# Pairing the chunks of a two-part matrix product so that its fp16 halves lie in runs of sixteen

## The chip, the core and the metric

The kernel runs on one core of a Trainium2 chip. Its time is the device time of one execution in microseconds, the median of several runs. The engines are named as in the profile: PE multiplies matrices (PEld is its loading of weights), DVE, ACT and POOL work on vectors, SP issues nearly all DMAs. Each engine works through its own list of instructions in order, and semaphores tie the lists together.

## The reference

The input x is 4 batches of 1024 tokens of 512 channels. It is normalized, and the result goes into two branches whose outputs are added to x:

```
xn  = layernorm(x)
# time mix, 704 hidden channels
k   = (xn + (shift(xn) - xn) * mix_k) @ Wk.T ;  r likewise with mix_r and Wr
s_t = s_(t-1) * exp(-exp(decay)) + relu(k_t) ;  a = layernorm((s * r) @ Wv.T) * gamma + beta
# feed-forward, 2048 hidden channels
d   = fp16(gelu(fp16(xn) @ W0.T + bias0)) ;     e = fp16(d @ W1.T + bias1)
out = x + a + e
```

## The kernel before

The tokens are cut into eight blocks of 512 (i = 0 to 7; block 1 is the second one). The tile of 128 x 512 is the unit of nearly all work.

**Feed-forward.** The hidden 2048 channels are 16 chunks of 128 (n = 0 to 15). For a chunk, `up` (L843) makes the hidden product pd, 512 columns wide, from four groups of input channels. The weights are in two parts, a high one in fp32r (w0h, against the inputs xf) and a low one in fp16 (w0l, against the fp16 inputs x16), so pd takes four fp32r and four fp16 products, in this order. ACT turns pd into d16 (gelu, L866) and copies it to d in fp32r (L869). `down` (L875) adds the chunk's share to the four output sums pe (one for each 128 tokens): four fp16 products of d16 with the low part of W1, then four fp32r products of d with the high part. The weights come back from DRAM in each block: w1 by `load_w1`, w0l by `load_w0l`.

**The loop.** Iteration n of a block runs, in this order on PE: `up` for the chunk two further on (its high, then its low products), `down` for chunk n (low, then high), and then a piece of the time mix. A piece is a three-pass product of k or r (L693 and L444: sums pa and pb, 12 products), a half pass (ph, 8 products) or, at n = 12 to 15, an output product for 128 tokens (`out_three_pass`, L790 to L800: sums oa and ob, 17 products). All of these are fp32r. So one iteration has 8 fp16 products in a row and else fp32r.

What follows a piece on DVE and ACT is emitted in the next iteration (`followers`): a<-pa on ACT (L705), y<-pb,a on DVE (L706), then the scan (L585) for k, or the gating g (L602) and the split of g into three parts hg, lg and mg (L278, L336, L338, L340) for r. An output piece is followed by oy (L805), its statistics, scaling and residual (L777, L782, L783). The gelu of the iteration is emitted between the first step of these works and the rest of them. Jobs of the next block are woven in between: its normalization and transposes, the mixing at n = 10, 12, 13 and 14 (L420, L424) and, behind each mixing, the split of the mixed inputs of one of the four channel groups into hk, lk and mk (`split_xk`). After iteration 15 DVE rounds the four sums pe to e (L833), which frees their banks of PSUM for the next block.

**Order and buffers.** Inside the loop the order of PE, DVE, ACT and SP is the order in which the code emits it. PSUM has four banks for pd, pa, pb, ph, oa and ob in turn, and four for pe. Nearly all tiles of SBUF come from one pool of equal buffers under the tag "q" (`part`, QS buffers): w0h, the parts h, l and m of the inputs, the states g and their parts, the parts of Wv. A new tile takes a buffer that an earlier one had, and its first writer waits for that tile's last reader. A few tags have their own buffers: kr (weights of the three-pass products, 6), w1 (2), w1l (2), w0l (2), d and d16 (3 each), xf (4), h16 (8).

**The tail.** The last block keeps the `down` of its last four chunks for the end: token groups 0 and 1 whole, 512 wide, groups 2 and 3 in two halves of 256 columns (`end_by_columns`, L886). There each fp16 product of a chunk is followed by its fp32r product.

Of the kernel before, what the change touches and what calls it, by code (L numbers as in the profile page):

```python
# [10 lines left out]
F16 = mybir.dt.float16  # L11
# [6 lines left out]
P = 128  # L18
# [4 lines left out]
def time_mix_and_gelu_ffn(  # L23
# [32 lines left out]
    nc = tc.nc  # L56
    B, T, C = x.shape
# [3 lines left out]
    NS = TB // P  # L61
    NC = C // P
    NN = N // P
    Q = 32
    QS = 62
    RAW_OUT = 1
    WV_FIRST = {0: 12, 1: 13, 2: 15, 3: 15, 5: 15}
    S = 4096.0
# [1 line left out]
    MASK = -4096  # L70
    OWN = dict(tag="q", bufs=QS)

# [5 lines left out]
    LAST = len(blocks) - 1  # L78
# [9 lines left out]

    def part(name, dtype=F32R, tag="q", bufs=QS):
        return wide.tile([P, TB], dtype, tag=tag, name=name, bufs=bufs)  # L90
# [112 lines left out]
    w0h, w0l, w0ls, w0l_pairs = {}, {}, {}, {}  # L203
# [18 lines left out]

    def load_w0l(i, n):
        if i > 1 or i == 1 and n >= G:
            w0ls[i, n] = part(f"w0l_{i}_{n}", F16, tag="w0l", bufs=2)
            g, k = divmod(n, G)
            src = w0l_dram[g][:, k].rearrange("p c k -> p (c k)")
            nc.sync.dma_start(w0ls[i, n], src)
# [19 lines left out]
    def load_w1(i, n):  # L248
        name = f"w1_{i}_{n}"
        if i == LAST and n >= NN - 2:  # L250
            w1 = [part(f"{name}_0"), pair(f"{name}_1")[0]]
        else:
            w1 = [
                part(f"{name}_0", tag="w1", bufs=2),
                part(f"{name}_1", F16, tag="w1l", bufs=2),
            ]
        if i == 0:
            split(*w1, w1_raw.pop(n))
        for p in range(2):
            sbuf, kept = as_stored(w1[p], p), as_stored(w1_dram[n][p], p)  # L260
            if i == 0:
                stores.append((kept, sbuf))
            else:
                nc.sync.dma_start(sbuf, kept)
        return w1
# [574 lines left out]
        queue.dma_start(out[b, rows, cols], z[:, cols])  # L840


    def up(i, n):  # L843
        pd = bank(f"pd_{i}_{n}")
        g, k = divmod(n, G)
        cols = slice(k * P, (k + 1) * P)
        low = w0ls.pop((i, n), None)
        for p in range(2):
            for c in range(NC):
                if p == 0:  # L850
                    w = w0h[c, g][:, cols]
                elif low is not None:
                    w = low[:, c * P : (c + 1) * P]
                else:
                    w = w0l[c, g][:, cols]
                nc.tensor.matmul(  # L856
                    pd, w, xf[c][p], start=(c == p == 0), stop=(c == NC - 1 and p == 1)
                )

        def after():  # L860
            if i == LAST and n >= NN - 2:
                d, d16 = part(f"d_{i}_{n}"), pair(f"d16_{i}_{n}")[0]
            else:
                d = part(f"d_{i}_{n}", tag="d", bufs=3)
                d16 = part(f"d16_{i}_{n}", F16, tag="d16", bufs=3)
            nc.scalar.activation(  # L866
                d16, pd, AF.Gelu, bias=b0_sb[:, n : n + 1], scale=1.0 / WS
            )
            nc.scalar.copy(d, d16)  # L869
            return d, d16  # L870

        return after


    def down(n, tiles, d, w1, first=0, end=lambda s: NN, sums=None, cols=slice(0, C)):  # L875
        for p in (1, 0):
            for s in tiles:
                nc.tensor.matmul(  # L878
                    (sums or pe)[s],
                    d[p][:, s * P : (s + 1) * P],  # L880
                    w1[p][:, cols],
                    start=(n == first and p == 1),
                    stop=(n == end(s) - 1 and p == 0),
                )

    def end_by_columns(s, chunks, base):  # L886
        first = NN - len(chunks)
        for half in range(2):
            cols = slice(half * C // 2, (half + 1) * C // 2)
            sum_ = bank(f"end_{s}_{half}")[:, : C // 2]  # L890
            for n, operands in chunks:
                down(n, [s], *operands, first=first, sums={s: sum_}, cols=cols)
            finish(LAST, s, rounded(LAST, s, sum_, cols, base), cols)

    AHEAD = 2
# [21 lines left out]
    def several(fn, *calls):  # L917
        for args in calls:
            fn(*args)

    engines = {e.engine for e in (nc.tensor, nc.vector, nc.scalar, nc.sync)}
    with tc.manual_schedule(engines=engines):
        for kind in range(2):
            begun[kind, 0] = begin_kr(kind, 0, lambda name: part(name, F32))
        first_x16(0)
        for h in range(FIRST):
            finished(raw_k(0, h, pks[h])())
        for c in range(1, NC):
            first_x16(c)
        xf = ffn_input(0)  # L930
        finished(raw_r(0, 0)())
        several(split_w0, (0, 0), (0, 1))
        finished(raw_r(0, 1)())
        several(split_w0, (0, 2), (0, 3))
        w1s = [load_w1(0, n) for n in range(AHEAD)]
        gated_last = raw_r(0, 2)
        several(split_w0, (1, 0), (1, 1))
        several(split_kr, (1, 0, 0), (1, 1, 0))
        finished(gated_last())
        waiting = []  # L940
        for n in range(AHEAD):
            waiting.append((up(0, n)(), w1s[n]))
            split_w0(1, 2 + n)
        store_weights()
    behind.close()

    followers = []
    e16s = []
    with tc.manual_schedule(engines=engines):
        for i in range(len(blocks)):  # L950
            j = i + 1
            tail = 4 if i == LAST else 0
# [106 lines left out]
            for n in range(NN):  # L1059
                ahead = n + AHEAD  # L1060
                if ahead == NN and j <= LAST:
                    xf = next_xf
                nxt = (i, ahead) if ahead < NN else (j, ahead - NN)
                gelu = up(*nxt) if nxt[0] <= LAST else None
                works = [follow() for follow in followers]
                works = [w for w in works if next(w, works) is None]
                several(scaled_now, *early[n])
                if i == 0 or n == out_at[0] or (n > out_at[0] and i < RAW_OUT):
                    finished(*works)
                    works = []  # L1070
                followers = []
                if gelu:
                    d = gelu()
                if ahead + 1 == NN and j <= LAST:
                    next_xf = ffn_input(j)
                if n < NN - tail:
                    operands = waiting.pop(0)
                    end = lambda s: NN - tail if s in by_columns else NN
                    down(n, range(NS), *operands, end=end)
                if gelu and i > 0:  # L1080
                    waiting.append((d, load_w1(*nxt)))
                two_on = (i, ahead + 2) if ahead + 2 < NN else (j, ahead + 2 - NN)
                if two_on[0] <= LAST:
                    load_w0l(*two_on)
                jobs = [
                    lambda s=s: finish(i - 1, s, e16s[s])
                    for s in (2 * n, 2 * n + 1)
                    if s < len(e16s)
                ]
                for work, *args in pieces[n]:  # L1090
                    followers.append(work(*args))
                if i == 0 and ahead + 2 < NN:
                    load_w1_raw(ahead + 2)
                woven(works, jobs + bg[n])
                if i == 0:
                    waiting.append((d, load_w1(*nxt)))
                    for job in behind_w1[n]:
                        job()
                if (i, n) == (1, 6):
                    stores.extend(late_stores)  # L1100
                store_weights()
# [4 lines left out]
    with tc.manual_schedule(engines={nc.tensor.engine, nc.vector.engine}):  # L1106
        chunks = list(zip(range(NN - tail, NN), waiting))
        bases = {}
        for s in by_columns:
            bases[s] = temp(f"base_{s}")  # L1110
            nc.vector.scalar_tensor_tensor(
                bases[s], pe[s], 1.0 / WS, b1_sb, ALU.mult, ALU.add
            )
        for s in range(NS):
            if s in by_columns:
                end_by_columns(s, chunks, bases[s])
                continue
            if s == 0:
                for some in (chunks[:-1], chunks[-1:]):
                    for whole in range(NS):  # L1120
                        if whole not in by_columns:
                            for n, operands in some:
                                down(n, [whole], *operands)
            e16 = rounded(LAST, s, pe[s])
            finish(LAST, s, e16, adder=nc.gpsimd, queue=nc.scalar)

# [42 lines left out]
```

## Time and profile before

| | |
|---|---|
| time, median of 3 runs | 856.82 us (856.69 to 857.08) |
| the profiled execution | 856.67 us, span 854.9 us |
| granted PE clock, mean | 0.999 |
| PE, DVE, ACT busy | 848.4, 681.3, 437.4 us |
| fp32r and fp16 products of `down` (L878), mean of one | 441 and 379 ns |
| high and low products of `up` (L856), mean of one | 397 and 382 ns |
| DMA | 168.29 MB, mean 197 GB/s |

The span is the time from the first to the last instruction of the profiled execution; all durations in the text are of that one execution. Matmuls overlap in the pipeline, so the step from one start to the next, not the duration of one, is what a product costs.

### The profile page before, as it was taken

Reading aid. Unit: us, or ns where it says so; the run is one execution under the profiler, and the core shown is the slowest. Engines: PE = TensorE matmul, PEld = TensorE weight load, DVE = VectorE, ACT = ScalarE, POOL = GpSimd, SP = SyncE. Lnnn points to the kernel's source line nnn. Section 1 sums busy time; section 2 is a strip of 40 time slices with the busy share of each in tenths; the row PEclk is TensorE's granted clock in tenths of the full one; section 3 lists DMA queues with packets and bytes.
Section 4 is the critical chain, followed back from the end, with each engine's and each line's share of the span. In section 5 each row is a group of like instructions: output and inputs, shape, how many; then the busy total and the mean of one; then the engine's idle time right before and its main releaser. Section 6 shows DMA issues by size and latency. Waiting matters only on the chain.

```text
span 854.9 us, 11164 instructions
## 1 busy us (share of the span) xinstructions
PE 848.4 (99%) x3748; PEld 586.7 (69%) x3748; DVE 681.3 (80%) x1112; ACT 437.4 (51%) x740; POOL 77.5 (9%) x145
## 2 busy tenths in 40 slices
PE   9999999999999999999999999999999999999998
PEld 7555546767776777676777677767677767777775
DVE  7689897898867988688887888788886898886547
ACT  5856764547444563544734456354553446544422
POOL 1100000000221002000021001100011200200002
PEclk9999999999999999999999999999999999999999
DMA  9977976664476644956548555584555855467523
GB/s 277 343 252 241 303 209 205 228 207 124 148 248 207 188 142 137 300 163 192 161 140 292 166 164 163 172 286 153 178 166 183 262 166 177 135 213 244 158 72 112
DMA packets 121621, 168.29 MB, mean 197 GB/s; under 512 B 21567, under 2 KB 57692, under 8 KB 121564
## 3 DMA queue, kind: packets, MB, share of 16 engines
q1 hardware_dynamic: 121116, 166.91, 61.7%
q10 hardware_dynamic: 448, 0.66, 0.3%
q8 instruction: 30, 0.49, 0.3%
q14 instruction: 27, 0.22, 0.1%
HBM read 142.88 MB, written 24.64 MB: 196 GB/s over the span
## 4 chain that ended last, share of the span: by engine, by line
PE 95%; DVE 3%; ACT 1%; DMA 1%; issue 0%; ACTq 0%
PE pd L856 25%; PE pe L878 25%; PE pa L693 15%; PE oa L790 7%; PE pb L444 7%; PE ob L798 4%; PE ph L722 3%; PE po L749 2%; PE pr L444 2%; PE ob L800 1%; PE pk L444 1%; PE pkr L667 0%; DVE stx L357 0%; DMA x<-in_L_attn_x 0%; DMA krd<-wt 0%
## 5 line engine op out<-in xcount | busy, mean ns | idle before, releaser
L878 PE MATMUL pe<-w,d 128*128 128x512 f16 x1008 | 245.1, 410 | 0.4 <-DVE w L200 0.4
L866 ACT ACTIVATE d<-pd,late_sb 128x512 f16<-128x512 f32 x128 | 87.7, 685 | 141.4 <-PE pd L856 141.2
L856 PE MATMUL pd<-xf,w0h 128*128 128x512 f32 x512 | 140.7, 397 | 0.0
L856 PE MATMUL pd<-x,w0l 128*128 128x512 f16 x512 | 132.8, 382 | 0.0
L878 PEld LDWEIGHTS pe<-w,d 128*128 128x128 f32 x504 | 95.2, 189 | 27.8
L856 PEld LDWEIGHTS pd<-xf,w0h 128*128 128x128 f32 x512 | 95.9, 188 | 25.4 <-issue 4.3
L706 DVE SCALAR_TENSOR_TENSOR y<-pb,a 128x512 f32<-128x512 f32 x70 | 48.4, 692 | 64.2 <-PE pb L444 62.5
L878 PEld LDWEIGHTS <-d 128*128 128x128 f16 x520 | 50.8, 98 | 62.0 <-issue 2.8
L705 ACT ACTIVATE a<-pa 128x512 f32<-128x512 f32 x70 | 41.8, 597 | 86.9 <-PE pa L693 84.6
L856 PEld LDWEIGHTS <-w0l 128*128 128x128 f16 x512 | 39.8, 98 | 63.7 <-issue 29.9
L869 ACT CAST d<-d 128x512 fp32r<-128x512 f16 x128 | 79.5, 621 | 4.0
L383 DVE STREAM_TRANSPOSE xnT<-x 32x512 f32<-32x512 f32 x112 | 78.6, 702 | 2.2
L351 POOL TENSOR_SCALAR ry<-mvy 128x1 f32<-128x1 f32 x32 | 18.9, 589 | 421.9 <-DVE mvy L358 421.9
L693 PE MATMUL pa<-lk,kr 128*128 128x512 f32 x140 | 54.7, 391 | 0.0
L790 PE MATMUL oa<-wv,lg 128*128 128x512 f32 x140 | 54.6, 390 | 0.0
L693 PE MATMUL pa<-hk,kr 128*128 128x512 f32 x140 | 54.6, 390 | 0.0
L790 PE MATMUL oa<-wv,hg 128*128 128x512 f32 x140 | 54.6, 390 | 0.0
L693 PE MATMUL pa<-lr,kr 128*128 128x512 f32 x136 | 53.1, 390 | 0.0
L693 PE MATMUL pa<-hr,kr 128*128 128x512 f32 x136 | 53.0, 390 | 0.0
L708 ACT ACTIVATE y<-y 128x512 f32<-128x512 f32 x35 | 22.1, 630 | 39.4 <-DVE y L706 39.4
L805 DVE SCALAR_TENSOR_TENSOR oy<-ob,oa 128x512 f32<-128x512 f32 x28 | 19.4, 692 | 23.0 <-PE ob L800 22.9
L444 PE MATMUL pb<-mk,kr 128*128 128x512 f32 x140 | 37.4, 389 | 0.0
(167 smaller groups left out, 1370.9 us busy)
## 6 DMA issues: line engine op xcount, KB each, us to landing
kr<-krd SPq DMA_DIRECT2D x207, 256.0 KB, 4.4
w<-w1d SPq DMA_DIRECT2D x112, 256.0 KB, 2.7
w<-w1d SPq DMA_DIRECT2D x112, 128.0 KB, 2.7
w0l<-w0d SPq DMA_DIRECT2D x108, 128.0 KB, 3.4
xres<-in_L_attn_x SPq DMA_DIRECT2D x32, 256.0 KB, 4.6
x<-in_L_attn_x SPq DMA_DIRECT2D x31, 256.0 KB, 5.4
krd<-wt SPq DMA_DIRECT2D x30, 256.0 KB, 2.3
out<-xres SPq DMA_DIRECT2D x28, 256.0 KB, 3.8
```

The lines of the kernel that those rows point to most:

```text
L383: nc.vector.transpose(dst[i * Q : (i + 1) * Q, :, :, j, :], src[j * Q : (j + 1) * Q, :, :, i, :],)
L444: return nc.tensor.matmul(dst, w[:, c, :], src, start=(c == 0), stop=(c == NC - 1))
L693: nc.tensor.matmul(pa, w[p][:, c, :], xs[j, c][p], start=(c == 0 and p == 0), stop=(c == NC - 1 and p == 1),)
L705: nc.scalar.activation(a, pa, AF.Copy, scale=1.0 + 1.0 / S)
L706: nc.vector.scalar_tensor_tensor(y, pb, -1.0 / S, a, ALU.mult, ALU.add)
L722: nc.tensor.matmul(pa, w[:, c].rearrange("p two k -> p (two k)"), xs[j, c][p], start=(c == 0 and p == 0), stop=(c == NC - 1 and p == 1),)
L790: nc.tensor.matmul(pa, gs[i, h][p][:, cols], wv[h][p], start=(h == 0 and p == 0), stop=(h == NF - 1 and p == 1),)
L798: nc.tensor.matmul(pb, gs[i, h][2][:, cols], wv[h][2], start=(h == 0), stop=False)
L856: nc.tensor.matmul(pd, w, xf[c][p], start=(c == p == 0), stop=(c == NC - 1 and p == 1))
L866: nc.scalar.activation(d16, pd, AF.Gelu, bias=b0_sb[:, n : n + 1], scale=1.0 / WS)
L869: nc.scalar.copy(d, d16)
L878: nc.tensor.matmul((sums or pe)[s], d[p][:, s * P : (s + 1) * P], w1[p][:, cols], start=(n == first and p == 1), stop=(n == end(s) - 1 and ...
```

## The change

From block 1 on chunks go in pairs. In an even iteration PE runs the high products of `up`, the high products of `down`, the piece, and at the end the low products of `up` and those of `down`. In the odd iteration after it, PE begins with the low products of `up` and `down`, and then come the high ones of both and the piece. So sixteen fp16 products lie in a row. The gelu of an even iteration is emitted in the next iteration, behind the first step of its works; that of an odd iteration at its end. Block 0 and the last four iterations of block 7 keep the order of before. In the tail the products go by part: for the whole groups all low ones of three chunks, then all high ones, then the last chunk likewise; for the halves the four low ones, then the four high ones. The pool "q" has two buffers fewer, w0l two more, and w1l one more.

```diff
-    QS = 62
+    QS = 60
...
-            w0ls[i, n] = part(f"w0l_{i}_{n}", F16, tag="w0l", bufs=2)
+            w0ls[i, n] = part(f"w0l_{i}_{n}", F16, tag="w0l", bufs=4)
...
-                part(f"{name}_1", F16, tag="w1l", bufs=2),
+                part(f"{name}_1", F16, tag="w1l", bufs=3),
...
+    HIGH_FIRST, LOW_FIRST = (0, 1), (1, 0)
...
+        def products(p, order=HIGH_FIRST):
             for c in range(NC):
...
+                    pd, weights(c, p), src[c][p],
+                    start=(c == 0 and p == order[0]),
+                    stop=(c == NC - 1 and p == order[1]),
...
-        return after
+        return products, after
...
-    def down(n, tiles, d, w1, first=0, end=lambda s: NN, sums=None, cols=slice(0, C)):
-        for p in (1, 0):
-            for s in tiles:
+    def down(
+        n, tiles, d, w1, p, order=LOW_FIRST, first=0, end=lambda s: NN, sums=None, cols=slice(0, C)
+    ):
+        for s in tiles:
...
-            for n, operands in chunks:
-                down(n, [s], *operands, first=first, sums={s: sum_}, cols=cols)
+            for p in LOW_FIRST:
+                for n, operands in chunks:
+                    down(n, [s], *operands, p, first=first, sums={s: sum_}, cols=cols)
...
-                gelu = up(*nxt) if nxt[0] <= LAST else None
+                paired = i > 0 and n < NN - tail
+                order = HIGH_FIRST if paired and n % 2 == 0 else LOW_FIRST
...
+                if not paired:
+                    hidden(0)
+                    hidden(1)
+                elif n % 2 == 0:
+                    hidden(0)
+                else:
+                    hidden(1)
+                    outputs(1)
+                    hidden(0)
                 works = [follow() for follow in followers]
                 works = [w for w in works if next(w, works) is None]
...
-                if gelu:
+                if behind_works:
+                    waiting.append(behind_works.pop()())
+                if gelu and not paired:
                     d = gelu()
...
+                if not paired:
+                    outputs(1)
+                outputs(0)
...
                 woven(works, jobs + bg[n])
...
+                elif paired and n % 2 == 0:
+                    hidden(1)
+                    outputs(1)
+                    behind_works.append(lambda gelu=gelu, w1=w1: (gelu(), w1))
+                elif paired:
+                    waiting.append((gelu(), w1))
...
-                    for whole in range(NS):
-                        if whole not in by_columns:
-                            for n, operands in some:
-                                down(n, [whole], *operands)
+                    whole = [s for s in range(NS) if s not in by_columns]
+                    for p in LOW_FIRST:
+                        for n, operands in some:
+                            down(n, whole, *operands, p)
```

`hidden(p)` runs `products` of the chunk two further on, `outputs(p)` runs `down` of chunk n, each for one part.

More of the change, by code (lines that the diff above doesn't have):

```diff
@@ L847, in up, with weights @@
         low = w0ls.pop((i, n), None)
-        for p in range(2):
-            for c in range(NC):
[L850 to L857, printed above, removed]
+        src = xf
+        def weights(c, p):
+            if p == 0:
+                return w0h[c, g][:, cols]
+            return w0l[c, g][:, cols] if low is None else low[:, c * P : (c + 1) * P]
+        def products(p, order=HIGH_FIRST):
+            for c in range(NC):
+                nc.tensor.matmul(
+                    pd,
+                    weights(c, p),
+                    src[c][p],
+                    start=(c == 0 and p == order[0]),
+                    stop=(c == NC - 1 and p == order[1]),
                 )
@@ L870, in after @@
             return d, d16
-        return after
-    def down(n, tiles, d, w1, first=0, end=lambda s: NN, sums=None, cols=slice(0, C)):
-        for p in (1, 0):
-            for s in tiles:
[L878 to L884, printed above, removed]
+        return products, after
[3 more added lines that the diff above has]
+        for s in tiles:
+            nc.tensor.matmul(
+                (sums or pe)[s],
+                d[p][:, s * P : (s + 1) * P],
+                w1[p][:, cols],
+                start=(n == first and p == order[0]),
+                stop=(n == end(s) - 1 and p == order[1]),
+            )
     def end_by_columns(s, chunks, base):
@@ L941, in time_mix_and_gelu_ffn @@
         for n in range(AHEAD):
-            waiting.append((up(0, n)(), w1s[n]))
+            products, gelu = up(0, n)
+            several(products, *[(p,) for p in HIGH_FIRST])
+            waiting.append((gelu(), w1s[n]))
             split_w0(1, 2 + n)
@@ L945, in time_mix_and_gelu_ffn @@
     behind.close()
-    followers = []
+    followers, behind_works = [], []
     e16s = []
@@ L1063, in time_mix_and_gelu_ffn, with hidden, outputs @@
                 nxt = (i, ahead) if ahead < NN else (j, ahead - NN)
-                gelu = up(*nxt) if nxt[0] <= LAST else None
+                paired = i > 0 and n < NN - tail
+                order = HIGH_FIRST if paired and n % 2 == 0 else LOW_FIRST
+                end = lambda s: NN - tail if s in by_columns else NN
+                products, gelu = up(*nxt) if nxt[0] <= LAST else (None, None)
+                def hidden(p):
+                    if products:
+                        products(p, order if paired else HIGH_FIRST)
+                def outputs(p):
+                    if n < NN - tail:
+                        down(n, range(NS), *operands, p, order, end=end)
+                if n < NN - tail:
+                    operands = waiting.pop(0)
+                if not paired:
[7 more added lines that the diff above has]
+                    hidden(0)
                 works = [follow() for follow in followers]
@@ L1075, in time_mix_and_gelu_ffn @@
                     next_xf = ffn_input(j)
[L1076 to L1079, printed above, removed]
+                if not paired:
+                    outputs(1)
+                outputs(0)
                 if gelu and i > 0:
-                    waiting.append((d, load_w1(*nxt)))
+                    w1 = load_w1(*nxt)
+                    if not paired:
+                        waiting.append((d, w1))
                 two_on = (i, ahead + 2) if ahead + 2 < NN else (j, ahead + 2 - NN)
```

## The prediction

> **What bounds the kernel now.** I read the page first (busy shares and the chain that ended last), then the PE timeline of single chunks, then the DVE, ACT and SP timelines at the places where the changed program's instruction order shows new waits. The page:
>
> ```profile
> PE 848.4 (99%) x3748; PEld 586.7 (69%) x3748; DVE 681.3 (80%) x1112; ACT 437.4 (51%) x740; POOL 77.5 (9%) x145
> ...
> PE 95%; DVE 3%; ACT 1%; DMA 1%; issue 0%; ACTq 0%
> ```
>
> PE is busy for 99% and is 95% of the chain, so a nanosecond saved or lost on PE is one of the time. The DVE has 80%: little room, and its work stands in one fixed order. The PE timeline of chunk n = 10 of block 3 (start, time, operation):
>
> ```profile
> 403.71 1.07 PE L856 MATMUL pd<-xf,w0h 128*128 128x512 f32 x4
> 404.62 1.04 PE L856 MATMUL pd<-x,w0l 128*128 128x512 f16 x4
> 405.50 1.95 PE L878 MATMUL pe<-w,d 128*128 128x512 f16 x8
> 407.28 0.39 PE L693 MATMUL pa<-hr,kr 128*128 128x512 f32 x1
> ...
> 410.01 1.07 PE L856 MATMUL pd<-xf,w0h 128*128 128x512 f32 x4
> ```
>
> One chunk is 6.30 us with 20 fp32r and 8 fp16 products. A chunk with an output piece has 25 and 8 and takes 7.43 (417.45 to 424.88), so one fp32r product is 1.13 / 5 = 0.2267. Single fp16 records start 0.2158 apart. 20 x 0.2267 + 8 x 0.2158 = 6.26; the 0.040 left over is the price of going from fp32r to fp16 and back once. The chunks of 16 + 8 (5.393 us) and 25 + 8 (7.433 us) leave 0.040 too.
>
> **Part 1, the pairs.** The order of PE does what the change says: 54 runs of sixteen fp16 products replace 108 runs of eight (48 pairs in blocks 1 to 6, 6 in block 7). 54 x 0.040 = 2.16 us less, all on the path. The other bound is the tail's row, where single products alternate: 8 pairs of fp16 and fp32r from 843.14 to 846.81 are 0.459 each, 0.017 over 0.2267 + 0.2158; by it the gain is 54 x 0.017 = 0.9. I take 0.040, measured in the very place. The Trainium skill ("TensorE: Matmul & The Clock Gate", the engine queue depth in its first table) has PE pull weight loads ahead of matmuls in flight, from which a change of type would cost nothing; by it this term is 0 and the sum 2.2 us higher. The rows (0.040 in every chunk) decide against it.
>
> **Part 2, the tail.** 512 wide: 8 alternating pairs become runs of 6, 6, 2 and 2, two round trips for eight: 8 x 0.459 = 3.67 becomes 8 x 0.4425 + 2 x 0.04 = 3.62, 0.05 less. 256 wide: 16 pairs in 3.93 us (846.81 to 850.74), 0.245 each, become runs of four. No row has fp32r products of 256 columns in a row; below, pure fp32 passes of 128 columns with a full weight load each step every 0.112; above, 0.245 less an fp16 half of 0.108 is 0.137. Four halves of 4 x 0.108 + 4 x (0.112 to 0.137) + 0.04 are 0.92 to 1.02 each against 0.98: 0.24 less to 0.16 more. I take 0.15 less. Tail: -0.2.
>
> **Part 3, what the pairs move.** In an even chunk the piece (three-pass, half or output products) starts after 8 fp32r products (1.81 us) instead of 16 (3.55), so its inputs are due 1.73 earlier; the hidden product's end goes behind the piece, its gelu (0.69) and copy (0.62) into the next chunk. In odd chunks gelu and copy go behind all other ACT work of the chunk. Set against the timestamps of before, every wait of PE in the loop keeps 0.8 us or more but those named below, most of them over 2: the bank that an even gelu must free is due 3.5 us into the next chunk and free at about 0.7; w1 and w0l loads keep 1.7 or more, and the new buffers (4 w0l, 3 w1l) keep SP from holding on them. Two places are not covered.
>
> First, block 1, n = 11 to 12, where the DVE also splits the last wv:
>
> ```profile
> 203.05 0.63 ACT L319 ACTIVATE wv<-vd 128x512 fp32r<-128x512 f32 x1
> 203.59 0.58 ACT L705 ACTIVATE a<-pa 128x512 f32<-128x512 f32 x1
> ...
> 206.11 0.62 ACT L336 CAST hg<-ug 128x512 fp32r<-128x512 f32 x1 [0.73 <-DVE ug L278]
> ```
>
> The odd chunk's gelu and copy (1.35) now stand between the first two lines, and the DVE's mg before that waits for a released buffer (0.9 later). a, y, g, ug and hg move from 206.73 to about 209.1. PE wants hg_4 at 202.97 + 1.81 + 8 x 0.2267 = 206.6. Cost 2.5 us, once; the same place in blocks 2 to 6 has 0.82 to spare and loses 0.3 of it. Bounds: 0 if the two delays hide behind the DVE's 0.45 of idle time and the mg wait does not bind, 2.5 if they add.
>
> Second, block 7, n = 2 (two pieces in one chunk). SP:
>
> ```profile
> 761.21 1.37 SPq L228 DMA_DIRECT2D w0l<-w0d  x1
> ...
> 763.63 1.45 SPq L330 DMA_DIRECT2D kr<-krd x3
> ```
>
> These three terms of kr (0, 3) land at 768.59, 769.26 and 769.91 by their records, just ahead of the products at 769.21. Now the products are due at 762.91 + 1.81 + 2.72 = 767.44: 1.6 late if SP issues as before, 0.4 to 0.6 if the w0l line takes 0.42 as its others do. I take 1.0.
>
> **Part 4, the buffers (QS 62 to 60).** This decides. In the changed program the DVE write of mk for the last channel group of the next block (L340, chunk n = 14) has a new wait: its buffer is that of the running block's hg_0, whose last reader is the first product of the fourth output piece, in chunk 15. It stands so in all six of blocks 1 to 6; before, the buffer was one whose readers were long done. The DVE at that place in block 3, and PE:
>
> ```profile
> 431.47 0.69 DVE L340 SCALAR_TENSOR_TENSOR mk<-lk,uk 128x512 fp32r<-128x512 f32 x1
> 432.59 0.69 DVE L805 SCALAR_TENSOR_TENSOR oy<-ob,oa 128x512 f32<-128x512 f32 x1 [0.42 <-PE ob L800]
> ...
> 435.78 0.75 DVE L782 SCALAR_TENSOR_TENSOR oy<-oy,ry,beta_sb 128x512 f32<-128x512 f32 x1 [0.77 <-POOL ry L352]
> 436.57 0.69 DVE L783 TENSOR_TENSOR xres<-xres,oy 128x512 f32<-128x512 f32 x1
> 437.18 2.48 DVE L833 SCALAR_TENSOR_TENSOR e<-pe,b_sb 128x512 f16<-128x512 f32 x4
> ```
>
> ```profile
> 432.31 1.07 PE L856 MATMUL pd<-xf,w0h 128*128 128x512 f32 x4
> ...
> 435.88 0.39 PE L790 MATMUL oa<-wv,hg 128*128 128x512 f32 x1
> ...
> 439.75 1.07 PE L856 MATMUL pd<-xf,w0h 128*128 128x512 f32 x4
> 440.66 1.04 PE L856 MATMUL pd<-x,w0l 128*128 128x512 f16 x4
> 441.53 1.95 PE L878 MATMUL pe<-w,d 128*128 128x512 f16 x8
> ```
>
> The oa at 435.88 keeps its place (an odd chunk still has 16 products ahead of its piece). It ends at 436.27, so mk starts at about 436.35 instead of 431.47, and everything behind it on the DVE, from the oy at 432.59 to the end of the four e<-pe at 439.66 (7.07 us, with a wait for POOL in it), starts when mk ends, at 437.07. The four e<-pe, which free the banks of pe, then end at 442.35, 442.95, 443.55 and 444.15. PE needs those banks for the next block's first outputs, and the pair order asks for them sooner: after 4 products (440.66), not 8 (441.53). The fourth output product could start at 440.66 + 3 x 0.2267 = 441.34 and starts at 444.2: PE loses 2.87 us. Before, the e<-pe had ended 1.9 ahead of even 441.53. Six block ends: 6 x 2.87 = 17.2 us. Bounds: 1.7 each if the later banks cost nothing beyond the first, 4.9 each if the whole lateness of the DVE comes through; I take the chain as rows give it, since the DVE idles 1.0 at 445.3 and 3.1 at 449.5 and catches up there.
>
> The same reuse delays a scan at n = 4 of blocks 2 to 6 by 2.4 us (it waits for the fifth k piece). The DVE has caught up by n = 6 and PE's tightest wait there, for d, keeps about 1.3: cost 0, up to 0.5 each if that cover is gone.
>
> **The sum.** -2.16 - 0.2 + 2.5 + 1.0 + 17.2 = +18.3. The profiled execution took 856.67 with a span of 854.9 (1.8 outside it); the median of the runs shown is 856.82, 0.15 above. Span 873.2, time 875.2. About 0.2% (1.7 us) is what a measurement of this kernel can tell from no change.
>
> **Rivals.**
> *The wait of mk never reaches PE* (faster). It decides at the last e<-pe: its end at 439.66 has 1.7 us in hand against 441.34. If mk is held less than that, because the buffer is free sooner than its last reader tells or something else takes the DVE's order apart, only the transitions count: 856.82 - 2.4 = 854.5, with the two small stalls up to 858. For it: PE waits 2.4 us in all in the trace of before, and the DVE has idle time. Against it: 4.9 is three times what is in hand. 7%.
> *The whole lateness comes through.* If the DVE does not catch up in n = 0 and 1 of the next block, each block end costs 4.9: 29.4 - 2.4 + 3.5 = +30.5, 887. Against it, the idle times named above. 8%.
> My forecast with its bounds has the remaining 85%. The range of 867 to 881 takes 1.5 to 3.9 us for each block end, and the single stalls at either bound. Chances: faster 0.05 and same 0.03, from the first rival, whose time is lowest when the small stalls are hidden as well; slower 0.92.
>
> The granted clock is 0.999 over the span, and no row has PE idle for 3 us in its middle, so I put no price on the clock. The Trainium skill (same page, Part 1) tells of half the clock after a window of about 3.4 us without work: by it, a window at half speed at each of six ends would be an estimated 6 x 1.7 = 10 us more, 885; no run here shows that, and PE's wait would come in pieces (1.7, then three of 0.4).
>
> **What would show it.** Right: in the waits of PE, pe <- DVE e at about 2.9 us for each of six block ends; in the DVE timeline, idle time of nearly 5 us before mk (L340), put down to PE oa, once a block; fp16 runs of sixteen with one 0.040 a pair; an idle PE of 2 to 3 us at n = 12 of block 1. Wrong: L340 in chunk 14 right behind lk, PE at 99% without waits, and a span near 852.5.

## The result, and the profile after

The changed kernel takes 876.09 us (median of 5 executions, 873.92 to 878.26) against 856.85 (856.69 to 857.08): slower, ratio 1.0226, 95% interval 1.0207 to 1.0245. The profiled execution took 876.96 with a span of 875.2. The forecast was 875.2, in a range of 867 to 881.

From the page, the busy time and the chain that ended last:

```profile
PE 857.4 (98%) x3748; PEld 594.1 (68%) x3748; DVE 677.3 (77%) x1112; ACT 434.4 (50%) x740; POOL 77.9 (9%) x145
...
PE 89%; DVE 6%; DMA 1%; ACT 1%; issue 1%; POOL 1%; SPq 0%; ACTq 0%
```

The DVE's share of the chain has doubled, from 3% to 6%: the chain now runs through the DVE at places where it ran through PE before. The busy time of PE rose by 9.0 us with the same 3748 products. This is not more work: 6.7 lies at the six block ends, where products that start 0.6 apart have records of 0.50 instead of 0.39, 2.0 lies ahead of the first `up`, and 1.6 is the half clock below. The waits (engine, line, waited for: us in total, times, longest):

```profile
DVE mk L340 <- PE oa L790: 29.9, 6, 5.1
...
PEld pe L886 <- DVE e L833: 18.6, 24, 1.9
...
PE pe L886 <- DVE e L833: 8.6, 6, 1.4
...
PE oa L790 <- ACT hg L336: 1.6, 1, 1.6
```

mk waits for an output product six times, once a block. PE's own wait for e is put down at 1.4 a time, half of what a block end costs: the other half lies inside the group of four products. The line of PEld shows it (4 loads at each of 6 ends). The DVE at the end of block 3; the first line is from block 1:

```profile
201.52 0.69 DVE L340 SCALAR_TENSOR_TENSOR mg<-lg,ug 128x512 fp32r<-128x512 f32 x1 [2.35 <-PE pa L693]
...
439.05 0.68 DVE L338 TENSOR_TENSOR lk<-xk,uk 128x512 fp32r<-128x512 f32 x1
444.58 0.69 DVE L340 SCALAR_TENSOR_TENSOR mk<-lk,uk 128x512 fp32r<-128x512 f32 x1 [4.84 <-PE oa L790]
445.19 0.68 DVE L805 SCALAR_TENSOR_TENSOR oy<-ob,oa 128x512 f32<-128x512 f32 x1
...
449.77 2.48 DVE L833 SCALAR_TENSOR_TENSOR e<-pe,b_sb 128x512 f16<-128x512 f32 x4
```

The DVE stands still for 4.84 us with work behind it, then runs through to e and catches up only 0.5 of it. PE at the same place and in the second pair of block 4; at the top the piece of n = 12 in block 1, at the bottom the tail:

```profile
209.74 0.50 PE L790 MATMUL oa<-wv,hg 128*128 128x512 f32 x1 [1.60 <-ACT hg L336]
...
444.15 0.39 PE L790 MATMUL oa<-wv,hg 128*128 128x512 f32 x1
...
448.00 1.07 PE L860 MATMUL pd<-xf,w0h 128*128 128x512 f32 x4
450.51 2.29 PE L886 MATMUL pe<-w,d 128*128 128x512 f32 x4 [1.44 <-DVE e L833]
...
463.42 1.07 PE L860 MATMUL pd<-xf,w0h 128*128 128x512 f32 x4
...
467.96 1.04 PE L860 MATMUL pd<-x,w0l 128*128 128x512 f16 x4
...
470.56 1.03 PE L886 MATMUL pe<-w,d 128*128 128x512 f16 x4
...
475.98 1.07 PE L860 MATMUL pd<-xf,w0h 128*128 128x512 f32 x4
...
863.90 3.75 PE L886 MATMUL pe<-w,d 128*128 128x512 f16 x16
867.49 3.86 PE L886 MATMUL end<-w,d 128*128 128x256 f16 x32
```

The four products of 450.51 last 2.29 where the same form takes 1.07 elsewhere: each starts as one of the four e<-pe ends, about 0.6 apart. Below, sixteen fp16 products lie in a row, and a pair of three-pass chunks takes 475.98 - 463.42 = 12.56; before it was 12.60.

### The profile page after: what moved, and what is told of

Read it like the earlier page. It is cut to its first block, busy times and chain, and to the rows that moved or that the text cites. A ratio compares the mean times of both kernels' runs of the same rounds, so it can differ in the third digit from the quotient of the medians.

```text
span 875.2 us, 11230 instructions
## 1 busy us (share of the span) xinstructions
PE 857.4 (98%) x3748; PEld 594.1 (68%) x3748; DVE 677.3 (77%) x1112; ACT 434.4 (50%) x740; POOL 77.9 (9%) x145
## 4 chain that ended last, share of the span: by engine, by line
PE 89%; DVE 6%; DMA 1%; ACT 1%; issue 1%; POOL 1%; SPq 0%; ACTq 0%
PE pd L860 24%; PE pe L886 24%; PE pa L693 14%; PE pb L444 7%; PE oa L790 6%; PE ph L722 3%; PE ob L798 3%; DVE e L833 2%; PE po L749 2%; PE pk L444 2%; PE pr L444 2%; PE ob L800 1%; DMA kr<-krd 1%; POOL ry L351 1%; DVE oy L782 1%
## 5 line engine op out<-in xcount | busy, mean ns | idle before, releaser
L886 PE MATMUL pe<-w,d 128*128 128x512 f32 (+1 forms) x1008 | 267.5, 391 | 10.8 <-DVE e L833 8.6
L860 PE MATMUL pd<-xf,w0h 128*128 128x512 f32 x512 | 151.7, 418 | 0.0
L860 PEld LDWEIGHTS <-w0l 128*128 128x128 f16 x512 | 44.1, 98 | 62.4 <-issue 16.9
L340 DVE SCALAR_TENSOR_TENSOR mk<-lk,uk 128x512 fp32r<-128x512 f32 x28 | 19.4, 692 | 31.0 <-PE oa L790 29.9
L336 ACT CAST hg<-ug 128x512 fp32r<-128x512 f32 x35 | 21.7, 620 | 41.3 <-DVE ug L278 41.0
```

Source lines behind the costliest of these rows:

```text
L860: nc.tensor.matmul(pd, weights(c, p), src[c][p], start=(c == 0 and p == order[0]), stop=(c == NC - 1 and p == order[1]),)
L886: nc.tensor.matmul((sums or pe)[s], d[p][:, s * P : (s + 1) * P], w1[p][:, cols], start=(n == first and p == order[0]), stop=(n == end(s) ...
```

## The experiments

The theory: the slowdown is the wait of mk at the block ends, the DVE works in order, and what it is late beyond 1.7 us reaches PE. Its rivals: the pairs themselves ask for the banks of pe too soon, the new buffers of w0l and w1l matter, or the buffer's late release counts wherever mk stands.

**The buffers alone, without pairs.**

```diff
 # the kernel before
-    QS = 62
+    QS = 60
```

> The kernel before with the pool q at 60 buffers instead of 62; PE's order is that of before, no pairs. Theory (the buffer decides): the DVE's mk of channel group 3 again waits for the first product of the fourth output piece in blocks 1 to 6, 4.8 us each, and the four e<-pe end 4.5 us late, at 442.35, 442.95, 443.55 and 444.15 on block 3's clock of before. PE asks for the fourth bank at 441.53 + 3 x 0.216 = 442.18, so it loses 1.97 us per block end, less than the 2.85 of the pairs because it asks 0.87 later: +11.8, about 868.7 (866 to 871). Rival (the pairs' earlier demand makes the stall, the buffers alone stay inside what is in hand): 857, no wait of PE for e. Rival (everything behind mk is late through the next block): 4.8 per block end, 885.

Measured: 867.65 against 856.64, ratio 1.013 (1.0115 to 1.0145). The wait of mk is there in the order of before. The waits, then PE at the beginning of block 4:

```profile
DVE mk L340 <- PE oa L790: 29.4, 6, 5.1
...
PE pe L878 <- DVE e L833: 7.2, 24, 0.5
```

```profile
444.20 1.07 PE L856 MATMUL pd<-xf,w0h 128*128 128x512 f32 x4
...
446.69 0.38 PE L878 MATMUL pe<-w,d 128*128 128x512 f16 x1 [0.54 <-DVE e L833]
447.28 0.38 PE L878 MATMUL pe<-w,d 128*128 128x512 f16 x1 [0.22 <-DVE e L833]
447.88 0.38 PE L878 MATMUL pe<-w,d 128*128 128x512 f16 x1 [0.22 <-DVE e L833]
448.48 1.30 PE L878 MATMUL pe<-w,d 128*128 128x512 f16 x5 [0.22 <-DVE e L833]
```

The four products follow the four e<-pe at steps of 0.6 instead of 0.22. The first chunk of blocks 2 to 7 takes 8.15 instead of 6.30: 1.85 lost, 1.97 expected, and six times that is the 11.0 of the timing. The buffers alone make most of the slowdown; the pairs add 1.0 to each end, most of it by asking 0.87 earlier.

**The pairs with one buffer more.**

```diff
 # the changed kernel
-    QS = 60
+    QS = 61
...
-            w0ls[i, n] = part(f"w0l_{i}_{n}", F16, tag="w0l", bufs=4)
+            w0ls[i, n] = part(f"w0l_{i}_{n}", F16, tag="w0l", bufs=3)
```

> The changed kernel with 61 buffers in q and 3 instead of 4 for w0l; pairs and tail as changed. Theory (the buffer decides): mk has no wait, PE's wait for e is gone, and what is left is -2.16 for 54 pairs, -0.3 for the tail, +2.4 at n = 12 of block 1 and +0.7 at n = 2 of block 7: about 857.5 (856.5 to 858.5), no difference from before. Rival (the pairs ask for pe too soon for the DVE at any buffer count): six waits of over 2 us stay, 870 or more. Rival (three w0l buffers make SP hold the loads behind it): PE waits for kr or w1, 858 to 862.

Measured: 856.86 against 856.64, ratio 1.0004 (0.9995 to 1.0014). No wait of PE for e is left, and no wait of mk for an output product. (In blocks 2 to 6 mk now waits up to 1.3 for a product pa inside the block, and PE loses nothing there.) By the trace the pairs still gain 0.040 each, and n = 12 of block 1 loses 1.83, n = 2 of block 7 0.63. So the pairs do not cost the block ends: with one buffer more in the pool, given up by w0l, the 17 us are gone.

**The pairs with all buffer counts of before.**

```diff
 # the changed kernel
-    QS = 60
+    QS = 62
...
-            w0ls[i, n] = part(f"w0l_{i}_{n}", F16, tag="w0l", bufs=4)
+            w0ls[i, n] = part(f"w0l_{i}_{n}", F16, tag="w0l", bufs=2)
...
-                part(f"{name}_1", F16, tag="w1l", bufs=3),
+                part(f"{name}_1", F16, tag="w1l", bufs=2),
```

> The changed kernel with all buffer counts of before: 62 in q, 2 for w0l, 2 for w1l. Theory: as with 61, about 857.5, if the loads of w0l, which now wait for the low products at the end of an even chunk, hold the kr loads behind them on SP by about 1 us and that stays hidden. If the new w0l and w1l buffers were needed: PE waits for w0l, w1 or kr, 859 to 866. Rival (pairs alone cost the block ends): 870 or more.

Measured: 860.29, ratio 1.0044 (1.0029 to 1.0059). The block ends are free here too, but the second rival has its share. The waits of PE:

```profile
PE pa L693 <- DMA kr<-krd: 1.9, 4, 1.2
```

Chunks 2 and 3 of block 7, where two pieces stand in one chunk, take 20.91, 3.8 more than the 17.13 they would without a wait; PE waits there for the kr terms. SP ahead of that place:

```profile
752.71 4.78 SPq L264 DMA_DIRECT2D w<-w1d  x2
757.54 1.52 SPq L228 DMA_DIRECT2D w0l<-w0d  x1
...
760.06 1.53 SPq L330 DMA_DIRECT2D kr<-krd  x3
```

In the version before this one, with three buffers for w1l, the same line of w1 loads takes 0.80 (from 751.94) and kr is issued at 754.25. With two, SP is held inside it for 4 us: the low part's buffer is read by the low products of `down`, which the pairs have moved to the end of the even chunk. I had looked at w0l for this; it is held too, by 1.1, but w1l holds SP longer. The stall at n = 12 of block 1 is 1.05 here, against 1.83 with 61 and 2.44 with 60: what depends on the size of the pool is 1.4 of it. The rest goes with the moved gelu: with 62 buffers the DVE has no wait for a buffer there, and y still waits 1.69 for a, which stands behind gelu and copy.

**The same 60 buffers, mk later on the DVE.**

```diff
 # the changed kernel; split_x keeps its last step back where later is set
-        nc.vector.scalar_tensor_tensor(m, l.bitcast(F32), -S, u, ALU.mult, ALU.add)
+        def third():
+            nc.vector.scalar_tensor_tensor(m, l.bitcast(F32), -S, u, ALU.mult, ALU.add)
...
+        if later:
+            late_m.append(third)
+        else:
+            third()
...
-        xks[i, c] = yield from split_x(xks[i, c], f"k_{i}_{c}")
+        xks[i, c] = yield from split_x(xks[i, c], f"k_{i}_{c}", i > 1 and c == NC - 1)
...
                 e16s = [rounded(i, s, pe[s]) for s in range(NS)]
+                while late_m:
+                    late_m.pop()()
```

> The changed kernel with its 60 buffers; only the place of the last mk changes: for channel group 3 it is emitted on the DVE behind the four e<-pe instead of in chunk 14, in the same buffer and with the same last reader. Theory (an in-order DVE behind one waiting instruction is the cost, not the buffer's lateness itself, since PE wants mk only some 4 us into the next block): the waits of PE for e are gone and mk waits for nothing, 857.5 (856.5 to 858.5). Rival (the buffer's late release is what counts, wherever mk stands): PE waits for mk or e at the block ends, 862 or more.

Measured: 857.57, ratio 1.0011 (1.0001 to 1.002). The DVE at the end of block 3:

```profile
438.50 2.48 DVE L842 SCALAR_TENSOR_TENSOR e<-pe,b_sb 128x512 f16<-128x512 f32 x4
440.89 0.68 DVE L344 SCALAR_TENSOR_TENSOR mk<-lk,uk 128x512 fp32r<-128x512 f32 x1
```

mk follows the last e<-pe at once, waits for nothing, and no wait of PE for e or for mk is left. The buffer is as late as in the changed kernel; only what stood behind the waiting instruction was the loss. The Trainium skill ("TensorE: Matmul & The Clock Gate", on queue depths in its section on the array) calls ACT and DVE strict FIFO. That agrees with the 4.84 us that the DVE stood still with oy ready.

**mk held for less, in two places.** In chunk 15 the wait is shorter, and less stands behind it. The scaling of an output piece, L777 of the changed kernel, is L791 here.

```diff
 # the version before, but mk as a job of chunk 15
-                while late_m:
-                    late_m.pop()()
...
+    def third_late():
+        for _ in range(2):       # two steps later: behind oy, statistics and scaling
+            yield
+        late_m.pop()()
...
+                if i > 0:
+                    put(15, third_late)
```

> The changed kernel with its 60 buffers, the mk of channel group 3 moved on the DVE from chunk 14 into chunk 15, behind oy, its statistics and its scaling (L777) and ahead of L782, L783 and the four e<-pe. It still waits for the first product of the fourth output piece. Theory (the DVE's lateness counts only beyond what is in hand): e is 3.1 less late than in the changed kernel, 1.4 late against the 1.7 in hand, so PE waits nothing for e although mk waits for PE in six blocks: 857.5 (856.5 to 859). Rival (any wait of mk for PE reaches PE in full): 1.4 for each block end, 866.

Measured: 858.10, ratio 1.0018 (1.0009 to 1.0027). Its waits, and its DVE at the end of block 3:

```profile
DVE mk L344 <- PE oa L804: 15.9, 6, 2.8
```

```profile
437.91 0.69 DVE L344 SCALAR_TENSOR_TENSOR mk<-lk,uk 128x512 fp32r<-128x512 f32 x1 [2.51 <-PE oa L804]
438.52 0.75 DVE L796 SCALAR_TENSOR_TENSOR oy<-oy,ry,beta_sb 128x512 f32<-128x512 f32 x1
...
439.91 2.48 DVE L847 SCALAR_TENSOR_TENSOR e<-pe,b_sb 128x512 f16<-128x512 f32 x4
```

The DVE waits 15.9 us in all for PE, and PE loses nothing at any block end. A wait that stays within the 1.7 in hand is free. Then the same without the two steps (`range(0)`), so that mk stands right behind oy:

> As the kernel with mk in chunk 15, but mk stands there right behind oy, ahead of its statistics, scaling and residual. Theory (lateness beyond what is in hand): against the changed kernel only oy, 0.61, no longer stands behind the wait, so each block end costs 2.85 - 0.61 = 2.24: 6 x 2.24 = 13.4 above the version with mk later (858.1), 871.5 (870 to 873.5). Rival (a wait of mk costs the same 2.85 wherever it stands): 875. Rival (the place behind oy is already early enough): 858.

Measured: 871.91 against 857.23, ratio 1.0181 (1.0166 to 1.0197). The DVE at the end of block 3:

```profile
441.99 0.69 DVE L344 SCALAR_TENSOR_TENSOR mk<-lk,uk 128x512 fp32r<-128x512 f32 x1 [4.24 <-PE oa L804]
...
446.45 2.47 DVE L847 SCALAR_TENSOR_TENSOR e<-pe,b_sb 128x512 f16<-128x512 f32 x4
```

The six block ends cost 2.09 to 2.13 by the trace, 2.24 expected. From one place to the next of the same instruction the cost goes 0, 0, 2.1, 2.85. Within 0.2 it is the lateness of e less what is in hand: at the end of block 3 the last e<-pe ends 1.30 us ahead of the next block's first product, then 1.05, 3.51 and 4.24 behind it, and the fourth output product is due 7 x 0.2267 = 1.59 behind it.

**What a change of type costs.** To measure the gain of the pairs from the other side, `down` ran its fp32r products first, so that a chunk goes fp32r, fp16, fp32r, fp16:

```diff
 # the kernel before, blocks 1 to 6
-        for p in (1, 0):
+        for p in order:          # (0, 1)
...
```

> The kernel before, but in blocks 1 to 6 `down` runs its fp32r products first and its fp16 products last, so that each of these 96 chunks goes fp32r, fp16, fp32r, fp16: two round trips in place of one. Same products, same buffers. Theory (each round trip costs 0.040): the chunk is 6.34 instead of 6.30, +3.84 in all, 860.7 (860.2 to 861.2). Rival (weights are pulled ahead, a switch is free, and the 0.040 belongs to something else in a chunk): 856.8, chunks of 6.30. Rival (0.017 as in the tail's alternating row): +1.6, 858.4.

Measured: 863.06 against 856.53, ratio 1.0076 (1.006 to 1.0091), without a new wait. One chunk of it:

```profile
400.04 1.07 PE L856 MATMUL pd<-xf,w0h 128*128 128x512 f32 x4
400.95 1.04 PE L856 MATMUL pd<-x,w0l 128*128 128x512 f16 x4
401.63 2.17 PE L880 MATMUL pe<-w,d 128*128 128x512 f32 x8
403.45 0.58 PE L693 MATMUL pa<-hr,kr 128*128 128x512 f32 x1
...
406.40 1.07 PE L856 MATMUL pd<-xf,w0h 128*128 128x512 f32 x4
```

It takes 6.367, not 6.34. A switch is not free: the rule of the Trainium skill ("TensorE: Matmul & The Clock Gate", the engine queue depth in its first table) that weight loads are pulled ahead of matmuls in flight does not make it so here. But my price was too low: two trips cost 0.107, not 0.080. Was it the short run of fp32r products between them? In a second version `up` ran its fp16 products first, so that eight fp32r products lie between:

```diff
 # the version above
+        order = (1, 0) if 0 < i < LAST else (0, 1)
-        for p in range(2):
+        for p in order:
...
```

> The kernel before, but in blocks 1 to 6 a chunk goes fp16 (`up`), fp32r (`up`), fp32r (`down`), fp16 (`down`), piece: again two round trips, with runs of four fp16 products, but now with eight fp32r products between them instead of four. The version with more switches took 6.367 for a chunk where 0.040 for a trip gave 6.34. Theory A (a trip next to a short run of four fp32r products costs more, otherwise 0.040): 6.34 for a chunk, +3.8, 860.5. Theory B (a trip with only four fp16 products costs more, whatever lies between): 6.367, +6.4, 863.0.

Measured: 862.91 against 857.04, ratio 1.007 (1.0053 to 1.0086), 6.366 for a chunk. A trip with four fp16 products costs 0.053, whatever lies between; one with eight or with sixteen costs 0.040, and single products that alternate in the tail of before cost 0.017. In these traces the steps between fp32r products are 0.224 to 0.239, most of them longer than the 0.2267 of a long run, for the next eight or so after fp16 ones. Why four are dearer than eight, and one cheaper, stays open.

**The tail alone.** The tail's new order, put into the kernel before:

```diff
 # the kernel before
+                    for p in (1, 0):
+                        for n, operands in some:
+                            down(n, whole, *operands, parts=(p,))
...
+            for p in (1, 0):     # the halves of 256 columns
+                for n, operands in chunks:
+                    down(n, [s], *operands, first=first, sums={s: sum_}, cols=cols, parts=(p,))
```

> The kernel before with the tail's new order alone: runs of 6, 6, 2 and 2 for the whole groups, runs of four for the halves. Theory: 512 wide 0.05 to 0.08 less, 256 wide 0.15 to 0.2 less, 856.6, too little to be told from no change by the time alone; by the trace the tail's products take 0.2 to 0.3 less. Rival (256-wide fp32r products in a row are bound by their weight loads): 0 to 0.2 more.

Measured: 856.22 against 856.53, ratio 0.9996 (0.9987 to 1.0005): the timing alone tells nothing. The trace does. PE in the tail:

```profile
844.33 3.75 PE L880 MATMUL pe<-w,d 128*128 128x512 f16 x16
847.92 3.86 PE L880 MATMUL end<-w,d 128*128 128x256 f16 x32
```

3.59 from the first to the second line in place of 3.67, and 3.86 in place of 4.07: 0.28 less, as in the changed kernel.

**Versions that are faster than both.** The two single stalls repaired, with 61 buffers:

```diff
 # the pairs with one buffer more
-                paired = i > 0 and n < NN - tail
+                paired = i > 0 and n < NN - tail and (i, n // 2) != (LAST, 1)
...
+                if (i, n) == (1, 11):
+                    waiting.append((gelu(), w1))
                 woven(works, jobs + bg[n])
...
-                elif paired:
+                elif paired and (i, n) != (1, 11):
                     waiting.append((gelu(), w1))
```

> The pairs with 61 buffers and 3 for w0l, and the two single stalls repaired: in block 1 the gelu of n = 11 is emitted ahead of that chunk's jobs, and chunks 2 and 3 of block 7 are left unpaired. Theory: 53 pairs x 0.040 = -2.1, tail -0.3, block 1 n = 12 keeps 0.5 of 1.8 (the 1.35 of gelu and copy go), block 7 n = 2 nothing: 854.9 (854.3 to 855.6), faster than both kernels. Rival (the stalls only move: the early gelu holds ACT's hg or hk, or the load of kr is late for the unpaired pair as well): 856 to 858.

Measured: 855.08 against 856.53, ratio 0.9983 (0.9974 to 0.9992). Block 7 has no stall left. At n = 12 of block 1 PE still loses 1.13 of 1.83 where 0.5 was expected: the earlier gelu takes only 0.7 away, since mg now waits 2.35 for its buffer and holds the DVE, where with the later gelu it was lk that waited 1.75. Then those chunks unpaired, which gives the piece its old place:

```diff
 # the pairs with one buffer more
+                plain = (i, n // 2) in ((1, 5), (1, 6), (LAST, 1))
-                paired = i > 0 and n < NN - tail
+                paired = i > 0 and n < NN - tail and not plain
```

> As the repaired pairs (61 buffers, 3 for w0l, chunks 2 and 3 of block 7 unpaired), but in block 1 chunks 10 to 13 are unpaired too instead of the earlier gelu, so that the piece of n = 12 again starts after 16 products. Theory: two pairs fewer cost 0.08, the 1.1 that the repaired version still lost at n = 12 of block 1 goes: 854.0 (853.5 to 854.6), 2.5 below before and faster than every version so far. Rival (the late mg of the smaller pool holds the piece in the old order as well): 0.5 to 1 stays, 854.6 to 855.1.

Measured: 854.15 against 857.23, ratio 0.9966 (0.9954 to 0.9979), 3.1 us faster. All waits of PE that this version has:

```profile
PE idle L461 <- PEq L1196: 0.8, 1, 0.8
PE pe L886 <- DVE w L200: 0.4, 1, 0.4
PE pt L488 <- DVE x L361: 0.2, 1, 0.2
```

They all lie ahead of block 1; 51 pairs and the tail are worth 51 x 0.040 + 0.28 = 2.3 by the trace, inside the interval of the timing (1.8 to 3.9).

## Why the prediction was right, step by step

| step of the prediction | forecast | by the trace |
|---|---|---|
| 54 pairs | -2.16 | -2.16 (12.560 for 12.600, 14.827 for 14.867) |
| tail | -0.2 | -0.28 |
| block 1, n = 12 | +2.5 | +2.44 |
| block 7, n = 2 | +1.0 | +0.71 |
| six block ends | +17.2 | +17.07 (2.83 to 2.86 each) |
| sum | +18.3 | +17.8 |

The profiled executions differ by 20.3. The other 2.5 are 1.59 of half clock in block 7 (below), 1.08 by which PE reached block 1 later, 0.98 of it ahead of the first `up`, in work that the change does not touch, and 0.17 less after the last product. No term of the prediction held these 2.5, while its own terms add up to 0.5 too much: that the median came within 0.9 of the forecast is in part luck. That the range held is not, since the block ends make 17 of the 18 and each link of them was measured.

**The pairs.** The trip price taken in the very place held to the nanosecond. The more-switches experiments show why that was the right row to take: the price is not the same elsewhere.

**The tail.** The 256-wide halves were mis-sized a little: 0.21 less, where 0.15 was taken between -0.24 and +0.16.

**Block 1.** Gelu and copy stand where the forecast put them. ACT in the changed kernel:

```profile
205.31 0.67 ACT L874 ACTIVATE d<-pd,late_sb 128x512 f16<-128x512 f32 x1
206.01 0.62 ACT L877 CAST d<-d 128x512 fp32r<-128x512 f16 x1
206.53 0.59 ACT L705 ACTIVATE a<-pa 128x512 f32<-128x512 f32 x1
...
209.07 0.62 ACT L336 CAST hg<-ug 128x512 fp32r<-128x512 f32 x1 [0.72 <-DVE ug L278]
```

hg ends at 209.69. PE reaches this chunk 0.84 later than before in this execution, so on the clock of before that is 208.85, against 209.1 in the forecast. The two delays add, as the upper bound had it: mg's wait, which shows at 201.52 above, moves wv by 0.88, and gelu and copy move a by 1.22 more (0.9 and 1.35 forecast). The list of waits has 1.60 of the 2.44 for hg. Another 0.40 went ahead of the piece's first product, which waited for the end of the late gelu; the prediction had not seen this, and it costs nothing of its own because the wait for hg is longer.

**Block 7.** The term was too large by 0.3, because SP does not issue as before: the kr line stands 0.2 ahead of the chunk's first product (782.93 against 783.15), 0.7 behind it before. The w0l line ahead of it takes 0.42, the lower case that the step had named. But 0.71 is the value of one execution. With kr issued at the same place of the chunk, PE lost 0.63 with 61 buffers, 1.19 with mk partly held and 0.03 with mk right behind oy: the first of the three terms landed 4.65 us into the chunk in the changed kernel, and 4.60, 5.18 and 3.85 in these, and it is due at 1.81 + 2.72 = 4.53. So agreement to 0.3 in this term is in part luck.

```profile
781.47 0.42 SPq L228 DMA_DIRECT2D w0l<-w0d  x1
...
782.93 1.89 SPq L330 DMA_DIRECT2D kr<-krd  x3
```

**The block ends.** Each link measured close to what it was to be. mk starts 0.43 behind the start of its oa (0.47 forecast), the last e<-pe ends 8.10 behind it (8.27), and PE loses 2.85 (2.87). The lateness ends there: the first pair of a block takes 15.41 in place of 12.56, the second 12.56 again, so the rival that the whole lateness comes through falls. The scans at n = 4 cost nothing, as said. One item of what would show it was read too simply: the waits of PE were to show 2.9 each, and the list shows 1.4, the rest being inside the group.

**The other rival**, that mk's wait never reaches PE, has the right threshold: with mk in chunk 15 behind L777 the DVE waits and PE does not.

## What to carry to other kernels

Before a reorder that pays in tens of nanoseconds, look at what pays for its buffers: here two buffers fewer in a shared pool turned one write into a wait, and an engine that works in order made seven microseconds of other work wait with it. Price such a wait by what stands behind it on its engine and by what is in hand at the point where the next engine needs it; moving the one instruction cost nothing here and was worth 18.5 us, more than the change could gain. Measure a small price (a change of type) at the place where it is to be saved, since it was 0.017, 0.040 and 0.053 in three places of one kernel and its versions.

## What the hardware showed beside this

After the sixth block end PE ran at half clock, though it never stood still for long. The windows of the changed kernel there (the stretch and its length in us; busy time and count of PE, PEld, DVE, ACT and POOL; the granted clock; DMA's share and GB/s):

```profile
766.00:768.00 2.00, 1.20 (x6) 0.66 (x4) 1.46 (x3) 0.00 (x0) 0.47 (x1) 1.00 0.00 0
768.00:770.00 2.00, 1.18 (x3) 0.54 (x3) 2.00 (x4) 0.00 (x0) 0.00 (x0) 1.00 0.00 0
770.00:771.00 1.00, 0.91 (x4) 0.51 (x5) 1.00 (x3) 0.00 (x0) 0.00 (x0) 1.00 0.00 0
771.00:774.50 3.50, 3.50 (x10) 2.73 (x9) 3.00 (x6) 0.39 (x1) 1.49 (x2) 0.51 0.66 225
```

The clock falls to 0.5 from about 771.1 to 774.5, behind one wait of 1.44 us and three short ones, and costs 1.59. The five other ends have the same waits and no such spell in this execution. The prediction put no price on the clock, and the five executions show about what that left out: spans of 872.1, 874.2, 874.3, 875.2 and 876.5 us go with mean clocks of 1.000, 0.998, 0.998, 0.997 and 0.996. In the version with mk right behind oy it is the same (867.4 at 1.000 to 872.1 at 0.995). Four executions of the buffers alone, whose waits are 0.5 at most, all have 1.000. The Trainium skill ("TensorE: Matmul & The Clock Gate", Part 1, the table of the two states and the text below it) gives half clock after at least one idle window of about 3.4 us, with a window that runs freely. The free-running window fits that only some of the ends are hit and that this spell lasts 3.4. An idle window does not fit: in the 3.4 us ahead of the fall (767.7 to 771.1) PE ran six products and was busy for 2.19 by the records, and in no stretch of that length there was it busy for less than about half. What share of idle time is enough no run here shows.
